# Low-rank conditional adapters: a closing product for every tile, or a fold into the heads' matrix for every batch

## The chip, the cores and the metric

The kernel runs on one core of one Trainium2 chip. The metric is the device time of one execution in microseconds; lower is better. Before the change the runs take 332.83, 332.95 and 333.03 us, with a median of 332.95. The engines are named as in the profile: PE (matrix products) and PEld (its weight loads), DVE (vector), ACT (scalar), POOL (GpSimd) and SP (the queue that issues most transfers).

## The reference

Eight batches of 512 rows, all in fp32. Each batch b has an adapter of rank 16, chosen by an index out of 32. The first layer is a full matrix plus bias plus the batch's adapter; the second routes each row to the best of 8 experts, each of rank 16. The cut code below leaves out how the inputs are drawn.

```
base_out = einsum('bti,oi->bto', x, W) + b            # W: 2048 x 2048
A, Bm = lora_As[adapter_mapping], lora_Bs[adapter_mapping]
y = base_out + 2.0 * einsum('btr,bro->bto', einsum('bti,bir->btr', x, A), Bm)

logits = einsum('bsd,ed->bse', y, route_w)            # 8 experts
topk_v, topk_idx = top_k(logits, 1)
weight = one_hot(topk_idx[..., 0], 8) * topk_v
h = einsum('bsd,erd->bser', y, A_ffn)                 # 8 x 16 = 128 columns
out = x + einsum('bser,eor->bso', weight[..., None] * h, B_ffn)
```

Only 136 columns of y are wanted, 128 of h and 8 logits, "the heads" in what follows. With proj the 2048 x 136 matrix of A_ffn and route_w, the heads of a row are x (W' proj) + b proj + 2 (x A)(Bm proj).

## The kernel before

**W stage (`chunk_w`, `fold_w`, loop over oc = 0 to 15).** W is loaded in 16 pieces of 128 rows. ACT and DVE bring each piece into blocks, and PE adds W' proj up in six PSUM tiles `pc` (3, 3, 3, 3, 3 and 1 blocks of 128 x 136). At oc = 15 the groups are copied, by ACT and DVE in turn, into the tiles `cms`. Between the pieces other work is put in by hand, in the order of the loop's `if oc == ...` lines: the adapters B are gathered by POOL (`load_adapters_b`), turned on PE in four groups (`turn_adapters`) and multiplied by proj (`project_adapters`, giving G, 128 x 136: 8 batches x 16 rows); G goes to DRAM and comes back in four copies into `g4`. The adapters A are gathered in four quarters (`load_adapters_a`), turned by DVE into `ad_aT`, and 16 columns of each batch are put beside W' proj by `place_a`. The first row tiles of x are loaded, moved in blocks (`shuffle`, on POOL and ACT) and turned by DVE (`turn_x`).

**Main loop (line 557).** There are 32 tiles of 128 rows, four to a batch, and each takes two iterations n, with t, h = divmod(n, 2). In each iteration the engines get this work, each in this order:

- PE: `heads` for half of the tile's 16 blocks of x, with the columns of `cms`: 16 of A and 136 of W' proj, 152 in all, into `ph`. Then `delta` for an earlier half tile (`piece(n)` is the half tile of n - 3): two products of 512 columns into one of two PSUM buffers `po`. In odd iterations then `add_low`, the closing product: the 16 columns x A of the tile, turned, times `g4`, added into `ph`; in even ones `turn_heads`, the transposition of the routed heads of the tile before.
- DVE: in even iterations `route` (five instructions on the 136 columns of the tile before, in PSUM); then `add_delta` for the half tile of the last iteration (x plus `po`, in place, 128 x 1024), `turn_x` for half of the next tile, and in odd iterations `turn_low`, which brings the 16 columns x A into four masked copies and turns them.
- ACT: in odd iterations `keep_heads`, the copy `whT` that `delta` multiplies; then its share of the moves of x for a later pair of tiles (`shuffle_slot`). POOL has the other moves, and once a batch `place_a` for the next batch but one.
- SP: the stores of finished tiles, and after them the load of the pair of tiles that takes the freed buffer. There are five buffers of two tiles.

An engine takes its work in the order in which it is written; semaphores between engines are set by the framework from the tiles read and written. PSUM has two buffers for `ph`, two of two banks for `po`, and two small ones (`ps_s`), which `pw` of `turn_heads` uses.

Of the kernel before, what the change touches and what calls it, by code (L numbers as in the profile page):

```python
# [9 lines left out]
F32 = mybir.dt.float32  # L10
# [8 lines left out]
def kernel(  # L19
# [28 lines left out]

    nc = tc.nc
# [19 lines left out]
    NA = NP + R  # L69
# [7 lines left out]
    dram = ctx.enter_context(tc.tile_pool(name="dram", bufs=1, space=bass.MemoryType.DRAM))  # L77
# [54 lines left out]
    for _ in range(14):  # L132
# [5 lines left out]
    quad_i = const.tile([P, NQ, 2], I32, name="quad_i")  # L138
    nc.gpsimd.iota(
        quad_i, pattern=[[1 - 2 * R * NQ, NQ], [-R * NQ, 2]], base=0, channel_multiplier=NQ  # L140
    )

# [14 lines left out]
    ad_ar = raw[:, 1, :].rearrange("p (k d) -> p k d", k=NQ)  # L157
# [3 lines left out]
    it_f = const.tile([P, B], F32, name="it_f")  # L161

    def load_adapters_b():

        nc.vector.tensor_scalar(it_f, it_i, float(R), None, ALU.mult)
# [3 lines left out]
        brow_f = const.tile([P, 1], F32, name="brow_f")  # L169
# [11 lines left out]
    def load_adapters_a():  # L181

        quad = const.tile([P, B], F32, name="quad")
        nc.vector.tensor_copy(quad, quad_i.rearrange("p i h -> p (i h)"))
        nc.vector.tensor_tensor(quad, quad, mask, ALU.mult)
        base = const.tile([P, 1], F32, name="base")
        nc.vector.tensor_reduce(base, quad, AX.X, ALU.add)
        odd = const.tile([P, 1], F32, name="odd")
        nc.vector.tensor_reduce(
            odd, mask.rearrange("p (i h) -> p h i", h=2)[:, 1, :], AX.X, ALU.add  # L190
        )
        it_q = const.tile([P, NQ, 2], F32, name="it_q")
        nc.vector.tensor_scalar(
            it_q, it_f.rearrange("p (k h) -> p k h", h=2), float(NQ), None, ALU.mult
        )
        arow_f = const.tile([P, NQ], F32, name="arow_f")
        nc.vector.tensor_tensor(arow_f, it_q[:, :, 1], it_q[:, :, 0], ALU.subtract)
        nc.vector.tensor_scalar(arow_f, arow_f, odd, base, ALU.mult, ALU.add)
        nc.vector.tensor_tensor(arow_f, arow_f, it_q[:, :, 0], ALU.add)
        arow_i = const.tile([P, NQ], I32, name="arow_i")  # L200
        nc.vector.tensor_copy(arow_i, arow_f)
        for m in range(NQ):
            nc.gpsimd.indirect_dma_start(
                out=ad_ar[:, m, :],
                out_offset=None,
                in_=cond_a.rearrange("s (i d) -> (s i) d", i=NQ),
                in_offset=bass.IndirectOffsetOnAxis(ap=arow_i[:, m : m + 1], axis=0),
            )

    one = const.tile([P, NQ, Q], F32, name="one")  # L210
    own4 = const.tile([P, NQ], F32, name="own4")
    hls = []

    def fill_constants():

        nc.vector.memset(one, 0.0)
        nc.vector.memset(one[:, :, R : R + 1], 1.0)

        nc.vector.tensor_reduce(
            own4, mask.rearrange("p (g h) -> p g h", h=2), AX.X, ALU.add  # L220
        )
        for k in range(2):
            h = const.tile([P, NQ, Q], F32, name=f"hls_{k}")
            nc.vector.memset(h, 0.0)
            nc.vector.tensor_copy(h[:, :, R : R + 1], own4.unsqueeze(2))
            hls.append(h)
# [5 lines left out]
    cms = [const.tile([P, n, NA + R], F32, name=f"cm_{n}") for n in (JC, NJ - JC)]  # L232

    def cm(j):
        return cms[j // JC][:, j % JC, :]

    def place_a(b, copy):
        for k, part in enumerate(cms):
            n = part.shape[1]
            copy(part[:, :, ds(b % 2 * NA, R)], ad_aT[:, ds(k * JC, n), ts(b, R)])  # L240

    ad_aT = const.tile([P, NJ, P], F32, name="ad_aT")
    ad_bT = tpool.tile([P, NJ, P], F32, tag="t", name="ad_bT")
    g4 = const.tile([P, B, NP], F32, name="g4")
    GRP = 512 // NP
    groups = [(j0, min(GRP, NJ - j0)) for j0 in range(0, NJ, GRP)]

    def turn(dst, src, h):

        nc.vector.transpose(  # L250
            dst[:, ts(h, HJ), :].rearrange("p j (g t) -> p g j t", t=Q),
            src.rearrange("p g (j a) -> p g j a", a=Q)[:, :, ts(h, HJ), :],
        )

# [48 lines left out]
    def fold_w(oc):  # L303
        for q, (pc, (j0, n)) in enumerate(zip(pcs, groups)):
# [11 lines left out]
            if oc == NO - 1:  # L316
                copy = nc.scalar.copy if q % 2 == 0 else nc.vector.tensor_copy
                copy(cms[j0 // JC][:, ds(j0 % JC, n), R:NA], pc[:, :n, :])

# [19 lines left out]
    g_dram = dram.tile([P, NP], F32, name="g_dram")  # L339

    def project_bias():

        pb = ps_s.tile([P, NP], F32, tag="s", name="pb")
        nc.tensor.matmul(
            pb, one.rearrange("p i s -> p (i s)"), bp, start=True, stop=True
        )
        nc.vector.tensor_copy(g4, pb.unsqueeze(1).to_broadcast([P, B, NP]))

    def project_adapters():
# [7 lines left out]
        nc.sync.dma_start(out=g_dram, in_=g_sb)  # L357
        for i in range(NQ):
            nc.sync.dma_start(
                out=g4[ds(i * Q, R)], in_=g_dram.rearrange("(b r) e -> r b e", r=R)  # L360
            )

    chunk_w(0)
    for oc in range(NO):
        if oc + 1 < NO:
            chunk_w(oc + 1)
        fold_w(oc)
# [6 lines left out]
        if 8 <= oc < 12:  # L374
            turn_adapters(oc - 8)
        if oc in (9, 10):
            fold_bias(range(8 * (oc - 9), 8 * (oc - 8)))
        if oc == 8:
            load_x(0)
            shuffle(0, moves[6:], nc.gpsimd.tensor_copy)  # L380
        if oc == 11:
            nc.sync.dma_start(out=fb, in_=ffn_b)
            load_x(1)
            load_x(2)
            project_bias()
        if oc in (10, 11):
            turn(ad_aT, ad_ar, oc - 10)
        if oc == 11:
            for b in range(2):
                place_a(b, nc.vector.tensor_copy)  # L390
        if oc == 12:
            project_adapters()
        if oc in (12, 13, 14):
            shuffle(0, moves[2 * (oc - 12) : 2 * (oc - 11)], nc.scalar.copy)
        if oc == 14:
            for h in range(2):
# [4 lines left out]
    xpool2 = ctx.enter_context(tc.tile_pool(name="xpool2", bufs=1))  # L401
    xpools.update({k: xpool2 for k in range(3, XB)})
# [3 lines left out]
    hT_tiles = {}  # L406
# [8 lines left out]
    def heads(t, j0, j1):  # L415
        s = batch_of(t) % 2
        if j0 == 0:

            pool, tag = (ps_h, "h") if t else (ps_s, "s")
            ph_tiles[t] = pool.tile([P, 512], F32, tag=tag, name=f"ph_{t}")[:, :NA]  # L420
        for j in range(j0, j1):
# [3 lines left out]
                cm(j)[:, ds(s * R, NA)],  # L425
# [4 lines left out]
    def turn_low(t):  # L430

        s = batch_of(t) % 2
        h = hls[t % 2]
        nc.vector.tensor_tensor(
            h[:, :, :R],
            ph_tiles[t][:, ds(s * NP, R)].unsqueeze(1).to_broadcast([P, NQ, R]),
            own4.unsqueeze(2).to_broadcast([P, NQ, R]),
            ALU.mult,
        )
        hT = small.tile([P, P], F32, tag="hT", name=f"hT_{t}")  # L440
        nc.vector.transpose(hT, h.rearrange("p g s -> p (g s)"))  # L441
        hT_tiles[t] = hT

    def add_low(t):
        b = batch_of(t)
        nc.tensor.matmul(  # L446
            ph_tiles[t][:, ds((1 - b % 2) * R, NP)],
# [199 lines left out]
```

## Time and profile before

| | before |
|---|---|
| median of the runs | 332.95 us |
| profiled execution | 332.04 us |
| its span, first to last instruction | 330.3 us |
| W stage, end of the last `pc` product | 72.4 us |
| PE busy from 81.01 to 316.24 us (235.23 us) | 235.23 us |
| heads, `ph` L422 | 1024 records, 142.6 us |
| closing products, `ph` L446 | 64 records, 12.7 us |
| DVE pair behind them, L434 and L441 | 32 x 188 ns, 32 x 311 ns |
| `route`, five lines | 167, 226, 162, 500 and 292 ns each |
| delta products, `po` L515 | 240 records, 112.8 us |
| granted PE clock | 0.999 |

A group's busy time is the time in which at least one of its instructions runs; matmuls overlap, so their single durations are longer than the distance from one to the next. The chain of waits follows the work that ended last from the end back to the start; where the chain stays on PE from one line to the next, PE had no gap there. "Released by" or an arrow names the instruction that ended an idle time.

### The profile page before, as it was taken

The page shows a single profiled execution, that of the slowest core. Times are in us where ns is not written, and L with a number is a line of the kernel's source. Part 1 is how long each engine was busy: PE and PEld are TensorE (multiplying, and loading weights), DVE is VectorE, ACT ScalarE, POOL GpSimd, SP SyncE. Part 2 cuts the span into 40 slices and gives each one's busy share as a digit, 9 for nine tenths or more (in the row PEclk, how much of TensorE's full clock was granted, in tenths as well). Part 3 has the DMA queues.
Part 4 walks back from the last instruction along what each step waited for, and adds up shares of the span by engine and source line. Part 5 has one row for each costly group of instructions (what it writes and reads, how often), then busy time and mean ns, then how long its engine had stood idle before and what let it go on. Part 6 is the DMA issues. An engine that isn't in the chain of part 4 may idle for free.

```text
span 330.3 us, 5132 instructions
## 1 busy us (share of the span) xinstructions
PE 324.2 (98%) x1968; PEld 260.8 (79%) x1968; DVE 234.3 (71%) x429; ACT 171.0 (52%) x193; POOL 136.7 (41%) x148
## 2 busy tenths in 40 slices
PE   8999999999999999999999999999999999999994
PEld 8999999998777777777777777777777777777762
DVE  1132376566877877887878888878888787787764
ACT  3234136647766538565656575667565665740000
POOL 1002403999882609264535536254808070700000
PEclk9999999999999999999999999999999999999999
DMA  7999999958643394857676675859493939433336
GB/s 286 347 409 418 419 406 424 419 220 342 270 167 131 119 386 157 360 179 329 217 293 243 267 279 229 297 215 359 167 372 168 373 153 383 191 127 129 128 159 222
DMA packets 16200, 88.83 MB, mean 269 GB/s; under 512 B 1824, under 2 KB 4784, under 8 KB 5936
## 3 DMA queue, kind: packets, MB, share of 16 engines
q1 hardware_dynamic: 14832, 85.80, 66.1%
q0 software_dynamic: 496, 2.11, 1.6%
q10 hardware_dynamic: 848, 0.61, 0.6%
q8 instruction: 15, 0.25, 0.3%
q14 instruction: 9, 0.07, 0.1%
HBM read 54.88 MB, written 33.62 MB: 268 GB/s over the span
## 4 chain that ended last, share of the span: by engine, by line
PE 94%; DMA 3%; SPq 0%; ACT 0%; DVE 0%; issue 0%; DVEq 0%; ACTq 0%
PE ph L422 40%; PE po L515 31%; PE pc L308 16%; DMA w<-in_w_dram 3%; PE ph L446 2%; PE pg L353 1%; PE pw L477 1%; PE pe_o L515 1%; PE pbT L335 1%; PE pe_h L515 1%; ACT wv L297 0%; DVE x L528 0%; PE pe_s L515 0%; SPq L102 0%; SPq L96 0%
## 5 line engine op out<-in xcount | busy, mean ns | idle before, releaser
L265 POOL COPY xq<-x 32x1024 f32<-32x1024 f32 x121 | 126.7, 1047 | 118.9 <-DMA x<-in_x_dram 67.6
L265 ACT COPY xq<-x 32x1024 f32<-32x1024 f32 x135 | 140.9, 1043 | 20.3 <-DMA x<-in_x_dram 11.0
L422 PE MATMUL ph<-cm,xT 128*128 128x152 f32 x1024 | 142.6, 293 | 0.0
L422 PEld LDWEIGHTS ph<-cm,xT 128*128 128x128 f32 x1024 | 135.1, 190 | 8.7 <-issue 8.7
L515 PE MATMUL po<-fb,whT 128*128 128x512 f32 x240 | 112.8, 592 | 0.0
L250 DVE STREAM_TRANSPOSE xT<-xq 128x1024 f32<-128x1024 f32 x64 | 78.8, 1235 | 0.9 <-POOL xq L265 0.9
L528 DVE TENSOR_TENSOR x<-x,po 128x1024 f32<-128x1024 f32 x60 | 72.6, 1210 | 5.2 <-PE po L515 5.0
L515 PEld LDWEIGHTS po<-fb,whT 128*128 128x128 f32 x240 | 42.0, 190 | 28.7 <-issue 28.7
L308 PE MATMUL pc<-pj,wv 128*128 128x136 f32 x512 | 60.7, 279 | 0.5 <-ACT wv L297 0.5
L308 PEld LDWEIGHTS pc<-pj,wv 128*128 128x128 f32 x512 | 59.8, 190 | 0.8 <-ACT wv L297 0.7
L482 ACT COPY whT<-pw 128x128 f32<-128x128 f32 x32 | 8.5, 266 | 85.8 <-PE pw L477 85.8
L297 DVE COPY wv<-w 128x1024 f32<-128x1024 f32 (+1 forms) x17 | 12.4, 737 | 31.2 <-DMA w<-in_w_dram 19.8
L297 ACT COPY wv<-w 128x1024 f32<-128x1024 f32 (+1 forms) x17 | 16.8, 997 | 27.9 <-DMA w<-in_w_dram 25.3
L459 DVE TENSOR_REDUCE top<-ph 128x1 f32<-128x8 f32 x32 | 5.3, 167 | 36.5 <-PE ph L446 36.5
L446 PEld LDWEIGHTS ph<-g,hT 128*128 128x128 f32 x64 | 12.0, 190 | 15.0 <-issue 11.7
L465 DVE TENSOR_SCALAR rw<-rank,win,top 128x8 f32<-128x8 f32 x32 | 16.0, 500 | 1.2
L446 PE MATMUL ph<-g,hT 128*128 128x136 f32 x64 | 12.7, 280 | 0.0
L173 POOL DMA_INDIRECT raw<-in_cond_b_dram,brow_i x1 | 1.5, 1462 | 24.3 <-DVE brow_i L172 24.3
L477 PEld LDWEIGHTS pw<-ident,wh 128*128 128x128 f32 x32 | 4.5, 140 | 7.9 <-issue 5.7
L441 DVE STREAM_TRANSPOSE hT<-hls 128x128 f32<-128x128 f32 x32 | 10.0, 311 | 1.1
L467 DVE TENSOR_TENSOR wh<-ph,rw 128x128 f32<-128x128 f32 x32 | 9.3, 292 | 1.1
L477 PE MATMUL pw<-ident,wh 128*128 128x128 f32 x32 | 8.8, 274 | 0.0
(69 smaller groups left out, 90.8 us busy)
## 6 DMA issues: line engine op xcount, KB each, us to landing
x<-in_x_dram SPq DMA_DIRECT2D x32, 1024.0 KB, 8.9
out_dram<-x SPq DMA_DIRECT2D x30, 1024.0 KB, 4.9
w<-in_w_dram SPq DMA_DIRECT2D x16, 1024.0 KB, 11.7
out_dram<-x SPq DMA_DIRECT2D x6, 256.0 KB, 2.6
fb<-in_ffn_b_dram SPq DMA_DIRECT2D x1, 1024.0 KB, 15.0
pj<-in_proj_dram SPq DMA_DIRECT2D x2, 272.0 KB, 11.0
g<-g_dram SPq DMA_DIRECT2D x4, 68.0 KB, 2.8
out_dram<-x ACTq DMA_DIRECT2D x1, 256.0 KB, 2.5
```

The lines of the kernel that those rows point to most:

```text
L250: nc.vector.transpose(dst[:, ts(h, HJ), :].rearrange("p j (g t) -> p g j t", t=Q), src.rearrange("p g (j a) -> p g j a", a=Q)[:, :, ts(h, ...
L265: copy(xq_tiles[u][ts(i, Q), :, g, :], x_tiles[u][ts(g, Q), :, ts(i, DQ)])
L297: copy(dst[:, ts(k, n)], wr[:, ds(h * HJ + k * n, n)])
L308: nc.tensor.matmul(pc[:, k, :], wv_tiles[oc, h][:, j, :], pj[:, oc, :], start=(oc == 0 and k == 0), stop=(oc == NO - 1), skip_group_check= ...
L422: nc.tensor.matmul(ph_tiles[t], xT_tiles[t][:, j, :], cm(j)[:, ds(s * R, NA)], start=(j == 0), stop=(j == NJ - 1),)
L441: nc.vector.transpose(hT, h.rearrange("p g s -> p (g s)"))
L446: nc.tensor.matmul(ph_tiles[t][:, ds((1 - b % 2) * R, NP)], hT_tiles.pop(t), g4[:, b, :], start=False, stop=True, skip_group_check=True,)
L465: nc.vector.tensor_scalar(rw, rank, win, top, ALU.is_equal, ALU.mult)
L467: nc.vector.tensor_tensor(wh.rearrange("p (e r) -> p e r", r=R), ph[:, :ER].rearrange("p (e r) -> p e r", r=R), rw.unsqueeze(2).to_broadca ...
L477: nc.tensor.transpose(pw, wh_tiles.pop(t), ident)
L515: nc.tensor.matmul(part, whT_tiles[t], fb[:, ds(c, n)], start=True, stop=True)
L528: nc.vector.tensor_tensor(xs, xs, part, ALU.add)
```

## The change

The adapters are no longer applied to every tile. For each batch the product A G is formed, 2048 x 136, and added to W' proj, so that the heads' matrix `ms[b % 2]` holds both: heads have 136 columns, and `turn_low`, `add_low` and the four masked copies go. W' proj is kept in `cs`. The bias' row is held in `c0b` and added by DVE as the first instruction of `route`, which now reads the sum `hl` in SBUF and stands in the odd iteration of its own tile.

A G has 16 terms, or 32 for a pair of batches with the other batch's rows of `g4` at nothing. So each of the 16 blocks is a product over 32 rows (`tile_position=(q * 32, 0)`), and A's blocks are spread over the four groups of rows (`spread_a`, 20 copies on POOL and 4 on ACT into `ad_q`); G is brought to all four groups by four products with an identity of 32 rows (`spread_g`), in place of the way through DRAM. `adapter_products` takes the groups of rows in turn, each with its own bank. For batch 0 this happens in the W stage in three bunches (`first_products`), and W' proj is added at oc = 15: ACT copies each group into `cs`, DVE adds it to `ms[0]`.

For batches 1 to 7 `fold_adapter` runs in the loop, in the odd iteration of the third tile of the batch before. Its 16 products use both `po` buffers and both small ones. DVE adds two pieces to `cs` straight out of PSUM; ACT copies four pieces out, and POOL adds `cs` to them. No `delta` is issued in that iteration; the next one issues two, and the `add_delta` of the first of them comes after `turn_x` on DVE. A is gathered whole by one gather in place of four.

```
     def load_adapters_a():
...
+        arow_i = const.tile([P, 1], I32, name="arow_i")
+        nc.vector.tensor_copy(arow_i, brow_f)
+        nc.gpsimd.indirect_dma_start(
+            out=ad_ar,
+            out_offset=None,
+            in_=cond_a,
+            in_offset=bass.IndirectOffsetOnAxis(ap=arow_i, axis=0),
+        )
...
+    half = const.tile([P, 2], F32, name="half")
+    def fill_constants():
         nc.vector.tensor_reduce(
-            odd, mask.rearrange("p (i h) -> p h i", h=2)[:, 1, :], AX.X, ALU.add
+            half, mask.rearrange("p (k h) -> p h k", h=2), AX.X, ALU.add
...
-        for m in range(NQ):
-            nc.gpsimd.indirect_dma_start(
-                out=ad_ar[:, m, :],
-                out_offset=None,
-                in_=cond_a.rearrange("s (i d) -> (s i) d", i=NQ),
-                in_offset=bass.IndirectOffsetOnAxis(ap=arow_i[:, m : m + 1], axis=0),
-            )
...
-    cms = [const.tile([P, n, NA + R], F32, name=f"cm_{n}") for n in (JC, NJ - JC)]
-    def cm(j):
-        return cms[j // JC][:, j % JC, :]
-    def place_a(b, copy):
-        for k, part in enumerate(cms):
-            n = part.shape[1]
-            copy(part[:, :, ds(b % 2 * NA, R)], ad_aT[:, ds(k * JC, n), ts(b, R)])
-    ad_aT = const.tile([P, NJ, P], F32, name="ad_aT")
+    parts = (JC, NJ - JC)
+    cs = [const.tile([P, n, NP], F32, name=f"c_{n}") for n in parts]
+    ms = {0: [const.tile([P, n, NP], F32, name=f"m0_{n}") for n in parts]}
+    ad_q = const.tile([P, NQ, 5, P], F32, name="ad_q")
+    def spread_a(q, k, copy):
+        src = ad_ar[ts(k, Q), :].rearrange("p (i j a) -> p j i a", i=NQ, a=Q)
+        dst = ad_q[ts(q, Q), k].rearrange("p j (i a) -> p j i a", a=Q)
+        copy(dst[:, :3], src[:, ds(3 * q, 3)])
+        if q < 2:
+            copy(dst[:, 3:], src[:, ds(JC + 2 * q, 2)])
...
+    eyes = const.tile([P, NQ, Q], F32, name="eyes")
+    nc.vector.tensor_reduce(
+        eyes[:, 0, :], ident.rearrange("p (q c) -> p c q", c=Q), AX.X, ALU.add
+    )
+    nc.vector.tensor_copy(eyes[:, 1:, :], eyes[:, :1, :].to_broadcast([P, NQ - 1, Q]))
...
-    def fold_w(oc):
+    def fold_w(oc, within=None):
         for q, (pc, (j0, n)) in enumerate(zip(pcs, groups)):
             for k in range(n):
...
             if oc == NO - 1:
-                copy = nc.scalar.copy if q % 2 == 0 else nc.vector.tensor_copy
-                copy(cms[j0 // JC][:, ds(j0 % JC, n), R:NA], pc[:, :n, :])
+                k, jk = divmod(j0, JC)
+                c, m = (part[k][:, ds(jk, n), :] for part in (cs, ms[0]))
+                nc.scalar.copy(c, pc[:, :n, :])
+                nc.vector.tensor_tensor(m, m, c, ALU.add)
+            if q == 2 and within:
+                within()
...
         pb = ps_s.tile([P, NP], F32, tag="s", name="pb")
-        nc.tensor.matmul(
-            pb, one.rearrange("p i s -> p (i s)"), bp, start=True, stop=True
-        )
-        nc.vector.tensor_copy(g4, pb.unsqueeze(1).to_broadcast([P, B, NP]))
+        nc.tensor.matmul(pb, warm, bp, start=True, stop=True)
+        nc.vector.tensor_copy(c0b, pb)
...
         nc.vector.tensor_scalar(g_sb, pg, COND_SCALING, None, ALU.mult)
-        nc.sync.dma_start(out=g_dram, in_=g_sb)
-        for i in range(NQ):
-            nc.sync.dma_start(
-                out=g4[ds(i * Q, R)], in_=g_dram.rearrange("(b r) e -> r b e", r=R)
+    def spread_g(ks):
+        for k in ks:
+            pq = ps_s.tile([P, NP], F32, tag="s", name=f"pq_{k}")
+            nc.tensor.matmul(
+                pq,
+                eyes[ts(k, Q)].rearrange("p q c -> p (q c)"),
+                g_sb[ts(k, Q), :],
+                start=True,
+                stop=True,
+                tile_position=(k * Q, 0),
             )
+            for h in range(2):
+                nc.vector.tensor_scalar(
+                    g4[:, 2 * k + h, :], pq, half[:, h : h + 1], None, ALU.mult
+                )
+    pieces = [(0, 3 * q, 3, q) for q in range(NQ)] + [(1, 2 * q, 2, q) for q in range(2)]
+    def adapter_products(b, some, banks):
+        for n in range(3):
+            for z in some:
+                part, _, nj, q = pieces[z]
+                if n < nj:
+                    nc.tensor.matmul(
+                        banks[z][:, n, :],
+                        ad_q[ts(q, Q), b // 2, 3 * part + n, :],
+                        g4[ts(q, Q), b, :],
+                        start=True,
+                        stop=True,
+                        tile_position=(q * Q, 0),
+                    )
+    def place(b, z):
+        part, j0, nj, _ = pieces[z]
+        return (t[part][:, ds(j0, nj), :] for t in (ms[b % 2], cs))
+    def first_products(some):
+        banks = {
+            z: ps_s.tile([P, GRP, NP], F32, tag="s", name=f"pa_{z}") for z in some
+        }
+        adapter_products(0, some, banks)
+        for z in some:
+            m, _ = place(0, z)
+            nc.vector.tensor_copy(m, banks[z][:, : pieces[z][2], :])
...
-        fold_w(oc)
+        fold_w(
+            oc,
+            {
+                13: lambda: spread_g((2, 3)),
+                14: lambda: first_products((2, 3)),
+            }.get(oc),
+        )
...
-        if 8 <= oc < 12:
-            turn_adapters(oc - 8)
+        for g in {8: (0,), 9: (1, 2), 10: (3,)}.get(oc, ()):
+            turn_adapters(g)
         if oc in (9, 10):
             fold_bias(range(8 * (oc - 9), 8 * (oc - 8)))
         if oc == 8:
             load_x(0)
+            for k in range(NQ):
+                for q in range(3):
+                    spread_a(q, k, nc.gpsimd.tensor_copy)
...
         if oc == 11:
+            for k in range(NQ):
+                spread_a(3, k, nc.scalar.copy)
...
-        if oc in (10, 11):
-            turn(ad_aT, ad_ar, oc - 10)
-        if oc == 11:
-            for b in range(2):
-                place_a(b, nc.vector.tensor_copy)
-        if oc == 12:
             project_adapters()
         if oc in (12, 13, 14):
             shuffle(0, moves[2 * (oc - 12) : 2 * (oc - 11)], nc.scalar.copy)
+        if oc == 12:
+            spread_g((0, 1))
+        if oc == 13:
+            first_products((0, 1))
         if oc == 14:
+            first_products((4, 5))
             for h in range(2):
                 turn_x(0, h)
...
     def heads(t, j0, j1):
...
             nc.tensor.matmul(
                 ph_tiles[t],
                 xT_tiles[t][:, j, :],
-                cm(j)[:, ds(s * R, NA)],
+                m[j // JC][:, j % JC, :],
                 start=(j == 0),
                 stop=(j == NJ - 1),
             )
-    def turn_low(t):
-        s = batch_of(t) % 2
-        h = hls[t % 2]
-        nc.vector.tensor_tensor(
-            h[:, :, :R],
-            ph_tiles[t][:, ds(s * NP, R)].unsqueeze(1).to_broadcast([P, NQ, R]),
-            own4.unsqueeze(2).to_broadcast([P, NQ, R]),
-            ALU.mult,
-        )
-        hT = small.tile([P, P], F32, tag="hT", name=f"hT_{t}")
-        nc.vector.transpose(hT, h.rearrange("p g s -> p (g s)"))
-        hT_tiles[t] = hT
-    def add_low(t):
-        b = batch_of(t)
-        nc.tensor.matmul(
-            ph_tiles[t][:, ds((1 - b % 2) * R, NP)],
-            hT_tiles.pop(t),
-            g4[:, b, :],
-            start=False,
-            stop=True,
-            skip_group_check=True,
-        )
...
     def route(t):
-        s = batch_of(t) % 2
-        ph = ph_tiles.pop(t)[:, ds((1 - s) * R, NP)]
+        hl = small.tile([P, NP], F32, tag="hl", name=f"hl_{t}")
+        nc.vector.tensor_tensor(hl, ph_tiles.pop(t), c0b, ALU.add)
         top = small.tile([P, 1], F32, tag="top", name=f"top_{t}")
-        nc.vector.tensor_reduce(top, ph[:, ER:NP], AX.X, ALU.max)
+        nc.vector.tensor_reduce(top, hl[:, ER:NP], AX.X, ALU.max)
...
+    def fold_adapter(b):
+        banks = {}
+        for z in range(0, 4, 2):
+            po = ps_o.tile([P, HN, 512], F32, tag="o", name=f"pa_{b}_{z}")
+            for k in range(2):
+                banks[z + k] = po[:, k, : GRP * NP].rearrange("p (j e) -> p j e", e=NP)
+        for z in (4, 5):
+            banks[z] = ps_s.tile([P, GRP, NP], F32, tag="s", name=f"pa_{b}_{z}")
+        adapter_products(b, range(4), banks)
+        adapter_products(b, (4, 5), banks)
+        for z in range(6):
+            m, c = place(b, z)
+            pa = banks[z][:, : pieces[z][2], :]
+            if z < 2:
+                nc.vector.tensor_tensor(m, c, pa, ALU.add)
+            else:
+                nc.scalar.copy(m, pa)
+        for z in range(2, 6):
+            m, c = place(b, z)
+            nc.gpsimd.tensor_tensor(m, m, c, ALU.add)
     def turn_heads(t):
         pw = ps_s.tile([P, P], F32, tag="s", name=f"pw_{t}")
@@ -554,43 +582,46 @@
         load_x(u)
     for n in (-2, -1):
         shuffle(*shuffle_slot(n), nc.gpsimd.tensor_copy)
+    def folds(n):
+        t, h = divmod(n, 2)
+        b, k = divmod(t, TPB)
+        return b + 1 if h == 1 and k == 2 and 0 <= b < B - 1 else None
...
-        if h == 0 and 0 < t <= NT:
-            route(t - 1)
         tp, hp = piece(n - 1)
-        if tp >= 0:
+        if tp >= 0 and not folds(n - 1):
             add_delta(tp, hp)
         turn_x(t + 1, h)
         if h == 1 and 0 < t <= NT:
             keep_heads(t - 1)
-        u, ms = shuffle_slot(n)
-        shuffle(u, ms, nc.gpsimd.tensor_copy if n == 2 else nc.scalar.copy)
+        if folds(n):
+            fold_adapter(folds(n))
         if h == 1 and t < NT:
-            turn_low(t)
-        last = n in (2 * NT - 1, 2 * NT)
...
+            route(t)
+        u, ms_u = shuffle_slot(n)
+        shuffle(u, ms_u, nc.gpsimd.tensor_copy if n == 2 else nc.scalar.copy)
+        if folds(n):
+            pass
+        elif n == 2 * NT:
+            delta(*piece(n), lambda: turn_heads(t - 1))
+        else:
+            if folds(n - 1):
+                delta(*piece(n - 1))
+                add_delta(*piece(n - 1))
+            if piece(n)[0] >= 0:
+                delta(*piece(n))
+            if n == 2 * NT - 1:
                 add_delta(*piece(n), 1)
-        elif piece(n)[0] >= 0:
-            delta(*piece(n))
-        if h == 1 and 0 < t < NT and not last:
-            add_low(t)
-        if h == 1 and t < NT:
-            b, k = divmod(t, TPB)
-            if k == 0 and 0 < b < B - 1:
-                place_a(b + 1, nc.gpsimd.tensor_copy)
-        if h == 0 and 1 < t <= NT and not last:
+        if h == 0 and 1 < t < NT:
             turn_heads(t - 1)
         tq, hq = piece(n - 5)
         u, k = divmod(tq, TPU)
```

## Prediction

> **What bounds the kernel now.** I read the page's first two parts (busy times, slices, granted clock), then a table of windows, then the chain of waits in order of time.
>
> ```profile
> PE 324.2 (98%) x1968; PEld 260.8 (79%) x1968; DVE 234.3 (71%) x429; ACT 171.0 (52%) x193; POOL 136.7 (41%) x148
> PEclk9999999999999999999999999999999999999999
> ```
> ```profile
> 81.01:316.24 235.23, 235.23 (x1276) 176.35 (x1276) 189.00 (x329) 136.40 (x153) 105.17 (x111) 1.00 0.61 238
> ```
>
> The columns of the second fence are window, length, busy time of PE, PE's weight loads, DVE, ACT and POOL, granted clock, DMA share, GB/s. From 81 us to 316 us PE is busy without a gap at the full clock, and DVE for 189 of 235 us. So a nanosecond of matmul counts in full, and nothing else counts until PE waits for it.
>
> ```profile
> 165.84 0.11 PE pw L477
> 165.95 2.07 PE ph L422 x16
> 168.02 1.72 PE po L515 x4
> 169.74 0.23 PE ph L446 x2
> 169.97 2.07 PE ph L422 x16
> 172.03 1.72 PE po L515 x4
> ```
>
> This is one row tile in the chain: 0.11 + 2.07 + 1.72 + 0.23 + 2.07 + 1.72 = 7.92 us. Eight products of the heads make 16 records: one fp32 matmul is two records, each with its own weight load. A record of 152 columns takes 2.07/16 = 0.129 us. The W stage is also solid PE work and gives the price at 136 columns:
>
> ```profile
> 53.87 3.71 PE pc L308 x32
> 57.57 3.71 PE pg L353 x32
> ```
>
> 3.71/32 = 0.116 us a record, 0.232 us a matmul.
>
> **What the change takes away.** Heads: 512 products, 1024 records, each 0.129 - 0.116 = 0.0132 us shorter: 13.5 us. Closing products: 32 x 0.23 = 7.4 us. Together **20.9 us** on PE, 0.65 us a tile. The DVE pair behind them goes too (188 + 311 ns by the groups), and one addition of 128x136 out of PSUM comes (like the 292 ns of the wh line): DVE falls from about 6.4 us a tile by 0.2, against a PE tile of 7.27 us. DVE doesn't become the bound on average.
>
> **What it adds on PE in the loop.** Seven times (batches 1 to 7) 16 products of 32 rows by 136 columns. No such product is in the trace. Dear end: each costs what a full one does, 16 x 0.232 = 3.71 us. Cheap end: four row groups run fully side by side; the pieces have 3, 3, 3, 3 and 2, 2 products, so five rounds, 5 x 0.232 = 1.16 us. In between: in every stretch of the trace PE's records stand in the order of the program, and the two records of one product use the same rows. If that order holds, the first record of a product can run beside the last of the one before, and no more: 17 x 0.116 = 1.97 us. I take **1.97 us**, because all rows here show records in order; 7 x 1.97 = 13.8 us (8.1 to 26.0).
>
> The Trainium skill has rules on both sides. "TensorE: Matmul & The Clock Gate", Part 3, gives a measured speedup of 3.07 for four row tiles at 512 columns; 3.71 us would become an estimated 1.21 us a batch, 5.3 us less over seven than my sum. The same page (LDWEIGHTS) says that a load of 32 rows takes as long as one of 128, which speaks for the dear end if loads take turns. "TensorEngine Tiling (Array Packing)", Key Properties, says that a change of tiling mode drains the array; that speaks against the change. No run here shows any of the three.
>
> Going into and out of these products may cost a stop. Bounds from rows: a product whose weight load isn't covered costs 0.16 us more than a covered one (the last transposition at 321.19 us, 0.27 against 0.11 us). Above, a 136-column record lasts 0.279 us in the groups and is followed after 0.116, so waiting for its end adds 0.163, and an uncovered load of 0.190 more: 0.35. The low end is nothing. I take **0.25 us** for each of 14 crossings: 3.5 us (0 to 4.9).
>
> **A new wait in the loop.** In the folding iteration, POOL gets four additions (two of 408, two of 272 columns) ahead of its last two moves of the next pair of tiles; ACT gets four copies out of PSUM ahead of its last two. Prices:
>
> ```profile
> L240 POOL COPY cm<-ad_aT 128x192 f32<-128x192 f32 x6 | 2.1, 344 | 0.4
> L318 ACT COPY cm<-pc 128x408 f32<-128x408 f32 x3 | 1.5, 500 | 4.8 <-PE pc L308 4.8
> L240 POOL COPY cm<-ad_aT 128x64 f32<-128x64 f32 x6 | 1.4, 231 | 0.0
> ```
>
> POOL's copies cost 0.175 us + 0.88 ns an element: 0.53 and 0.41 us for 408 and 272. Additions read two tensors. Cheap end: the copies' price, 1.9 us for the four; dear end: twice, 3.8 us. Count from E, the end of the products. ACT's first copy is done at E + 0.2 (its product ended before E), the last at E + 1.6. POOL's additions then end between E + 2.1 and E + 4.05, its two moves (1.05 us each) between 4.2 and 6.15. Only then can DVE turn the next tile (1.24 us), and in this iteration the addition of the postponed delta (1.21 us) stands behind that turn on DVE: done between E + 6.75 and E + 8.7. That addition frees the PSUM buffer which PE wants for the delta of the iteration after. PE has by then one crossing, heads, two deltas, a transposition and heads: 0.25 + 1.85 + 3.44 + 0.11 + 1.85 = E + 7.5. So PE waits 0 to 1.2 us. I take the additions nearer the dear end, since no row has POOL read two tensors at the price of one: **1.0 us** a batch, 7.0 us (0 to 8.4). Behind that turn on DVE stand also the next deltas and the routing; DVE has a fifth of its time free and catches up in two iterations.
>
> "GPSIMD Engine Reference" in the Trainium skill says that additions of two inputs run at about half of VectorE's rate on that engine and gives 4497 ns for 2048 fp32 columns; that would be an estimated 3.0 us for the four, and a wait of some 0.4 us, 2.8 us in all where I have 7.0. No run here shows it.
>
> **What it adds before the loop.** That stage is solid PE too. 4 spreading and 16 folding products in five bunches, pairs of row groups: by the in-between rule 20 x 0.116 + 5 x 0.116 = 2.9 us (2.3 for ten rounds of 0.232; 4.6 for 20 single ones). Ten crossings: 2.5 us (0 to 3.5). At its end heads wait for six ACT copies and now six DVE additions of SBUF tensors. After the fourth group PE has four products left, 0.93 us, against 0.50 (ACT) + 0.58 (DVE's 408-column copy): 0.2 us late. But POOL moves x all this time, and DVE's W copy goes from 0.69 to 1.53 us then:
>
> ```profile
> 33.38 0.69 DVE L297 COPY wv<-w 128x1024 f32<-128x1024 f32 x1 [3.01 <-PE pc L308]
> ...
> 58.35 1.53 DVE L297 COPY wv<-w 128x1024 f32<-128x1024 f32 x1
> ```
>
> I take **1.0 us** (0.2 to 2).
>
> **At nothing.** POOL's 20 spreading copies: 12 x 0.51 + 8 x 0.40 = 9.3 us. POOL waits for x until 54.99 us anyway; the A gather was last seen landing at 50.5, so x's moves slip by 5 us at most, to 71.7, and the first turn to 74.1, with PE's fold ending at 72.4 + 5.4 = 77.8. Without that cover each microsecond would delay the first heads by as much. ACT's four spreads (about 2 us) stand in an iteration in which it is busy for 1.6 of 3.7 us. DVE loses two turns and five placing copies (some 5 us) and gains 8 spreads, 6 copies and the sum of two masks, about 6 us in a stage where it is busy 28 of 58. The bias products and the 16 transpositions only move. On the queues: SP loses the store of G and four loads that stood ahead of x's tiles 3 and 4 (72.48 to 74.30 us), POOL three of four gathers of the same bytes; x's loads gain up to 2 us there. In the loop the narrowest place is ACT's moves at 282.22 us, which waited for x and ended 2.1 us before PE would have missed whT; four iterations shorter by 0.33 us leave 0.8 us.
>
> **Sum.** -13.5 - 7.4 + 13.8 + 3.5 + 7.0 + 2.9 + 2.5 + 1.0 = **+9.8 us**. The profiled execution took 332.04 us (span 330.3 and 1.7 around it); the median of the runs is 332.95. By the sum the profile of after has a span near 340.1 and the median is **342.7 us**. Within the case, no crossing cost and no POOL wait give 329.7; the dear ends of both and of the startup 347.5.
>
> **Rivals.** *The row groups take turns.* Products at 3.71 a batch and 4.6 before the loop: 12.2 + 1.7 = 13.9 us more, 356.6; without the POOL wait 349.6. For it: two weight loads to each short product, and no row with two products at once. Against: weight loads already overlap products in all of the trace.
>
> *Four at a time, faster.* Products at 1.16 and 2.3: five rounds. With the additions cheap enough for POOL's chain to end before E + 7.5: -20.9 + 8.1 + 3.5 + 2.3 + 2.5 + 1.0 = -3.5 us, **329.4 us**. It decides below a price of a folded batch of (20.9 - 2.3 - 2.5 - 1.0)/7 = 2.2 us on PE, crossings and waits included; full overlap and two crossings are 1.66. For it: pieces go to four different banks and to rows that don't touch. Against: the two records of a product follow each other.
>
> *Pairs, but POOL not late.* The forecast without its wait: **335.7 us**; for it, POOL is idle for 59% and its moves before the additions run ahead.
>
> **How the numbers follow.** Forecast 0.36 (342.7), turns 0.30, four at a time 0.20, pairs without a wait 0.14. The measurement tells about 0.2%, 0.7 us, from no change. Faster: 0.17 of the four (the rest for its having the wait) and 0.06 of the two cases of pairs with cheap crossings: 0.23. Same: 0.05. Slower: 0.72. Range 327.5 to 354: it takes in the fast case and its crossings below my value, and most of the dear one; 330 to 347.5 is the forecast's own.
>
> **What will show it.** The folding products' records and the gap from heads to the next heads: 2 us (pairs), 1.2 (four), 3.7 (turns). PE idle beside them: crossings. A PE wait for a DVE addition to x two iterations later, with POOL's additions and moves ahead of the DVE turn: the new wait. Heads at 1.85 us for 16 records. I am wrong above all if a folded batch costs PE less than 2.2 us, or if another engine (ACT with whT, x's landing) holds PE in most tiles.

## Result and profile after

The changed kernel takes 341.14 us (median; 339.94 to 342.87) against 332.89 before: a ratio of 1.0252 with a 95% interval of 1.0204 to 1.03, **slower by 8.2 us**. The profiled execution took 340.57 us, its span is 338.5 against 330.3. The page's first part, and one window of the loop, with the columns as in the prediction:

```profile
PE 321.7 (95%) x2168; PEld 253.3 (75%) x2168; DVE 253.8 (75%) x410; ACT 184.1 (54%) x228; POOL 165.6 (49%) x180
PEclk9999999999999999999999999999999999999999
```
```profile
169.70:327.10 157.40, 152.47 (x949) 111.49 (x950) 136.09 (x209) 91.26 (x114) 77.62 (x78) 1.00 0.62 241
```

PE has less work than before (321.7 against 324.2 us busy) and yet ends later: in the loop, where it had no gap, it is now idle for 4.9 of 157.4 us at the same full clock. The list of what PE waited for (total us, times, longest) names the places:

```profile
PE po L543 <- DVE x L556: 7.7, 7, 1.1
PE pw L505 <- DVE wh L472: 2.1, 2, 1.5
PE ph L452 <- DVE m L297: 1.1, 3, 0.4
```

Seven waits of 1.1 us for a DVE addition to x: one for each folded batch. The other two rows stand at the start of the loop, but for one wait of some 0.5 us for `wh` at 119 us, after the first fold. The chain of waits goes through one fold so:

```profile
158.53 1.86 PE ph L452 x16
160.38 0.98 PE pa L361 x24
161.38 0.51 ACT m L498
162.03 3.55 POOL m L501 x4
165.66 1.01 POOL xq L242
166.71 1.05 POOL xq L242
167.82 1.13 issue
168.95 1.19 DVE x L556
170.28 1.96 PE po L543 x4
```

The heads take 1.86 us for 16 records, as predicted for 136 columns. The products' first 24 records take 0.98 us. Then the chain leaves PE: ACT's first copy, POOL's four additions (3.55 us), POOL's two moves of x behind them, DVE's turn (here "issue", 1.13 us; DVE's rows have it from 167.78 to 169.03), DVE's delayed addition, and only then the delta. By POOL's and DVE's groups:

```profile
L501 POOL TENSOR_TENSOR m<-m,c 128x408 f32<-128x408 f32 x14 | 14.4, 1052 | 49.0 <-ACT m L498 42.9 <-issue 6.1
L501 POOL TENSOR_TENSOR m<-m,c 128x272 f32<-128x272 f32 x14 | 10.7, 786 | 0.0
L297 DVE TENSOR_TENSOR m<-m,c 128x408 f32<-128x408 f32 x5 | 4.8, 1020 | 0.0
L472 DVE TENSOR_TENSOR wh<-hl,rw 128x128 f32<-128x128 f32 x32 | 20.7, 648 | 1.1
L466 DVE SCALAR_TENSOR_TENSOR key<-hl,top,rank 128x8 f32<-128x8 f32 x32 | 11.2, 350 | 1.1
```

POOL's additions are at the dear end of the prediction (2 x 1.05 + 2 x 0.79 = 3.68 us; 3.8 said). Three DVE instructions are slower than the rows they were priced by: the 408-column additions at the end of the W stage (1.02 us; 0.58 for the copies of before), and the routing's last product and comparison (648 and 350 ns; 292 and 226 before). DVE's busy time rises from 234.3 to 253.8 us.

**Where the 8.2 us of span went.** A batch in the loop takes 31.89 us (heads of the folding tile at 158.53 us, of the next at 190.42) against 31.64 before. The part before the first heads is 4.9 us longer (they start at 72.2 before; the fold of W ends near 77.1 now). From there to the heads of the third tile takes 13.0 us (77.1 to 90.1) against 10.6 before, though 1.3 us of heads and closing products are gone: a loss of 3.75 us (the last kernel below takes 9.24, 77.09 to 86.33). The rest is in the loop.

### The profile page after: what moved, and what is told of

Same layout as the page of the kernel before. It is cut to its first block, busy times and chain, and to the rows that moved or that the text cites. A ratio compares the mean times of both kernels' runs of the same rounds, so it can differ in the third digit from the quotient of the medians.

```text
span 338.5 us, 5603 instructions
## 1 busy us (share of the span) xinstructions
PE 321.7 (95%) x2168; PEld 253.3 (75%) x2168; DVE 253.8 (75%) x410; ACT 184.1 (54%) x228; POOL 165.6 (49%) x180
## 4 chain that ended last, share of the span: by engine, by line
PE 64%; POOL 13%; DVE 10%; issue 6%; DMA 5%; ACT 1%; POOLq 0%; DVEq 0%; ACTq 0%
PE ph L452 23%; PE po L543 21%; PE pc L285 13%; POOL m L501 7%; POOL xq L242 5%; DVE x L556 4%; DMA w<-in_w_dram 3%; PE pa L361 2%; DVE xT L220 2%; DMA pj<-in_proj_dram 2%; DVE m L297 1%; PE pg L330 1%; PE pe_o L543 1%; ACT m L498 1%; PE pw L505 1%
## 5 line engine op out<-in xcount | busy, mean ns | idle before, releaser
L452 PEld LDWEIGHTS ph<-m,xT 128*128 128x128 f32 x1024 | 125.0, 190 | 20.0 <-issue 14.0
L452 PE MATMUL ph<-m,xT 128*128 128x136 f32 x1024 | 130.2, 280 | 1.1 <-DVE m L297 1.1
L556 DVE TENSOR_TENSOR x<-x,po 128x1024 f32<-128x1024 f32 x60 | 71.4, 1199 | 3.8 <-PE po L543 3.6
L501 POOL TENSOR_TENSOR m<-m,c 128x408 f32<-128x408 f32 (+1 forms) x28 | 24.8, 919 | 49.0 <-ACT m L498 42.9
L472 DVE TENSOR_TENSOR wh<-hl,rw 128x128 f32<-128x128 f32 x32 | 20.7, 648 | 1.1
L498 ACT COPY m<-pa 128x408 f32<-128x408 f32 (+1 forms) x28 | 10.4, 457 | 17.6 <-PE pa L361 17.6
L470 DVE TENSOR_SCALAR rw<-rank,win,top 128x8 f32<-128x8 f32 x32 | 18.9, 592 | 1.2
L361 PE MATMUL pa<-g,ad_q 32*128 32x136 f32 x256 | 12.7, 288 | 0.0
L466 DVE SCALAR_TENSOR_TENSOR key<-hl,top,rank 128x8 f32<-128x8 f32 x32 | 11.2, 350 | 1.1
L361 PEld LDWEIGHTS pa<-g,ad_q 32*128 32x128 f32 x256 | 10.6, 184 | 1.3
```

Source lines behind the costliest of these rows:

```text
L361: nc.tensor.matmul(banks[z][:, n, :], ad_q[ts(q, Q), b // 2, 3 * part + n, :], g4[ts(q, Q), b, :], start=True, stop=True, tile_position=(q ...
L452: nc.tensor.matmul(ph_tiles[t], xT_tiles[t][:, j, :], m[j // JC][:, j % JC, :], start=(j == 0), stop=(j == NJ - 1),)
L470: nc.vector.tensor_scalar(rw, rank, win, top, ALU.is_equal, ALU.mult)
L472: nc.vector.tensor_tensor(wh.rearrange("p (e r) -> p e r", r=R), hl[:, :ER].rearrange("p (e r) -> p e r", r=R), rw.unsqueeze(2).to_broadca ...
L498: nc.scalar.copy(m, pa)
L501: nc.gpsimd.tensor_tensor(m, m, c, ALU.add)
```

## Experiments

**One: the moves of x ahead of the fold.** In the folding iteration POOL and ACT have their moves for the next tiles before the products, where they waited for PE anyway.

```
         if folds(n):
+            u, ms_u = shuffle_slot(n)
+            shuffle(u, ms_u, nc.scalar.copy)
             fold_adapter(folds(n))
...
-        u, ms_u = shuffle_slot(n)
-        shuffle(u, ms_u, nc.gpsimd.tensor_copy if n == 2 else nc.scalar.copy)
+        if not folds(n):
+            u, ms_u = shuffle_slot(n)
+            shuffle(u, ms_u, nc.gpsimd.tensor_copy if n == 2 else nc.scalar.copy)
```

> The folding iteration's last moves of x (two on ACT, two on POOL) are issued ahead of the fold's products, copies and additions; nothing else changes. Theory (POOL's two moves stand behind its four additions, so DVE's turn and the delayed addition behind it come late, and PE waits 1.1 us plus an uncovered weight load of 0.2 in each of seven batches): the PE waits on the delayed addition go from 7.7 us in all to under 1, and the time falls by 8 to 9 us, to about 332.5 us. Rival (the wait comes from DVE having too much in that stretch, whatever POOL does): the waits shrink by less than a third and the time stays above 338. Rival (ACT's two moves ahead of its copies now hold up the PSUM buffers): PE waits for ACT copies appear and most of the gain is lost, 337 to 341.

Measured: 330.47 us (330.38 to 330.75), a ratio to before of 0.9941 (0.9930 to 0.9953). The waits of the delta on DVE are gone from the list. The chain of waits through the same fold:

```profile
155.31 1.86 PE ph L452 x16
157.16 1.36 PE pa L361 x32
158.52 2.05 PE ph L452 x16
160.57 3.43 PE po L543 x8
164.00 0.11 PE pw L505
164.12 1.86 PE ph L452 x16
165.97 1.72 PE po L543 x4
```

The chain stays on PE. POOL's additions are as long as ever (3.54 us in its rows) and nobody waits for them. So the order of a few instructions was worth 10.7 us by the medians (341.14 to 330.47), 9.9 us by the profiled spans (338.5 to 328.6), and turned the change from a loss into a gain of 0.6%. Of the 9.9 us, the seven waits with the uncovered weight load beside each make 9.3 (7 x 1.33, worked out under three); the 8 to 9 us expected left out the wait after the first fold, which went too. No ACT wait took the place of the old one.

**Two: the same wait cut on DVE.** POOL stays late, but the addition no longer stands behind the turn.

```
-        turn_x(t + 1, h)
+        if not folds(n - 1):
+            turn_x(t + 1, h)
...
                 add_delta(*piece(n - 1))
+                turn_x(t + 1, h)
```

> Only in the iteration after a fold, DVE's turn of the next tile is put behind the addition of the postponed delta; POOL keeps its additions ahead of its moves. Theory (it is the order on DVE that lets a late POOL reach PE): the addition no longer waits for POOL, the PE waits of 7.7 us go to under 1.5, time about 332.5 to 333.5 us, though POOL's additions and moves end as late as before. Rival (the turn is needed as early as it stood; what is late is the turn itself, by way of the next heads): the wait of PE moves from the delta to heads on the turned tile, and the time stays above 338.

Measured: 333.22 us (332.26 to 334.56), ratio to before 1.0025 (1.0012 to 1.0038). DVE's timeline after a fold (start, length, instruction, in brackets the idle time before it and who ended it):

```profile
163.07 1.22 DVE L556 TENSOR_TENSOR x<-x,po 128x1024 f32<-128x1024 f32 x1 [0.59 <-PE po L543]
165.31 1.25 DVE L220 STREAM_TRANSPOSE xT<-xq 128x1024 f32<-128x1024 f32 x1 [1.02 <-POOL xq L242]
```

DVE still waits 1.02 us for POOL, but with the addition done before, PE doesn't. So both links are needed for the loss: POOL late, and the delayed addition behind the turn. This cure leaves a batch at 30.75 us (products at 157.91 and 188.66) against 30.57 (157.16 and 187.73) with the first one, which is 1.3 us over seven batches; the medians are 2.75 us apart, and the rest of that was not followed up.

**Three: no folds in the loop.** `folds` returns None and all tiles use `ms[0]`: the adapters of batches 1 to 7 are left out.

> Leaves out the folds of batches 1 to 7: all tiles are multiplied by the matrix of batch 0, and the loop has the deltas in their usual place. It prices all that a fold costs. Theory (1.5 us of products and crossings and 1.3 us of waiting a batch): 7 x 2.8 = 20 us less than the changed kernel, about 321 us, with a tile of 7.26 us in the loop. Rival (the loop lost time by its other rearrangements too, such as the routing in the odd iteration): the loop's tile stays above 7.5 us and the time above 327.

Measured: 319.44 us, one run. From 170 to 310 us PE is busy throughout:

```profile
170.00:310.00 140.00, 140.00 (x786) 101.44 (x785) 122.94 (x193) 80.23 (x92) 58.07 (x56) 1.00 0.67 260
```

A batch takes 29.01 us (heads at 151.84 and, four tiles on, at 180.85). So in this stretch nothing else in the new loop holds PE. With the 30.56 us of a batch in the first experiment (155.31 to 185.87), a fold's **products and crossings cost 30.56 - 29.01 = 1.55 us, and the wait 31.89 - 30.56 = 1.33 us**.

**Four to six: the order of the products.** First, piece by piece in the changed kernel:

```
-        for n in range(3):
-            for z in some:
+        for z in some:
+            for n in range(3):
```

> The 16 products of a fold (and those of batch 0) are ordered piece by piece, so that neighbours use the same 32 rows, apart from the change of piece. Theory (four row groups run side by side because neighbours use different rows; 24 records take about 1.0 us): by the piece order the records run one after another, 32 x 0.116 less some overlap at the five changes of piece, 3.1 to 3.7 us a batch in place of 1.4; PE time of the products rises by 12 to 16 us over seven batches and by 1 to 2 in the W stage, part of it given back by a shorter wait on POOL (up to 6 us), time 347 to 354 us. Rival (a product over 32 rows is simply shorter than one over 128): records stay at 0.04 us apart, time unchanged within 2 us of 341.

Measured: 347.26 us, one run. The time fell inside the range, at its low edge, but neither number of its working did: the products took 2.04 us, neither 3.1 nor 1.36, and the waits grew from 7.7 to 9.6 us in place of shrinking. The counts of records that touch a window of 0.06 us show it, first for the kernel after, then for this one (window, length, PE busy, count in brackets):

```profile
160.54:160.60 0.06, 0.06 (x8) 1.00 0.64 273
160.77:160.83 0.06, 0.06 (x12) 1.00 0.64 273
160.89:160.95 0.06, 0.06 (x12) 1.00 1.29 546
```
```profile
162.57:162.63 0.06, 0.06 (x4) 1.00 1.29 546
162.86:162.92 0.06, 0.06 (x6) 1.00 1.93 819
163.15:163.21 0.06, 0.06 (x7) 1.00 1.93 819
```

A record lasts 0.274 us, and full products, one after another, show 3 in such a window. In the changed kernel 12 are under way, four times as many: four products at a time. Ordered by pieces there are 6 to 7, about two at a time. Since the wait on POOL blurs the time, two orders were run again on the first experiment's kernel: by pieces, and the first four pieces in two pairs.

```
-        adapter_products(b, range(4), banks)
+        adapter_products(b, (0, 1), banks)
+        adapter_products(b, (2, 3), banks)
```

> The kernel with the moves ahead of the fold (330.5 us, 1.36 us for a fold's 32 records), with the products ordered piece by piece, so that neighbours mostly use the same 32 rows. With no wait on POOL left, the time shows the price of the order alone. Theory (PE starts a record whose rows are free although one before it in the program still waits for its own rows, but sees only a short way ahead; 2.04 us a fold in the earlier run of this order): 0.7 us x 7 more in the loop and 0.5 to 1 us in the W stage, 335.5 to 336.5 us. Rival (strict program order, overlap only where the piece changes, 27 steps of 0.116): 3.1 us a fold, 12 us more in the loop, above 342.

> The kernel with the moves ahead of the fold, with the first four pieces in two pairs (products of pieces 0 and 1 in turn, then of 2 and 3): neighbours use different rows, but only two groups of rows stand near one another in the program. Theory (PE sees some records ahead, so the second pair starts before the first is through): between 1.4 and 1.7 us a fold, 331 to 333 us. Rival (only what stands next in the program can run beside: two at a time, 6 + 6 + 4 steps of 0.116 in place of 6 + 4): 2.0 us a fold, 335 us.

Measured: by pieces 335.39 us (335.24 to 335.51), 4.9 us more than with all four in turn; in pairs 330.66 us (330.52 to 330.81), the same. Both are a little under their ranges (335.5 and 331). The chain of waits has a fold, by pieces and then in pairs, as below; the third view counts records in a window of the fold in pairs.

```profile
189.60 2.04 PE pa L361 x31
```
```profile
187.52 1.36 PE pa L361 x27
```
```profile
188.22:188.28 0.06, 0.06 (x12) 1.00 1.93 819
```

(The chain does not pass through all 32 records.) With pairs in turn, strict program order would allow two at a time and 16 steps of 0.116, 1.9 us; PE does it in the 1.36 us of four, and here too 12 records are under way at once. So it starts products on free rows that stand some places further on in the program; in this, PE is an exception to the sentence, given with the kernel before, that an engine takes its work in the order in which it is written. How far it looks was not measured; six records of one piece in a row are too many for full overlap.

**Seven: the start of the loop.**

```
-                nc.vector.tensor_tensor(m, m, c, ALU.add)
+                nc.vector.tensor_tensor(m, m, pc[:, :n, :], ALU.add)
...
-            first_products((4, 5))
             for h in range(2):
                 turn_x(0, h)
+            first_products((4, 5))
```

> At the end of the W stage DVE adds each group of W' proj to the first matrix straight out of PSUM (not from ACT's copy in SBUF), and turns x's first tile ahead of the last two copies of products. Theory (the start of the loop lost 3.7 us: the additions took 1.02 us each, not 0.58, because both operands lay in SBUF while POOL moved x, and they stood behind the turns; heads and then the first transposition waited for DVE): additions near 0.58 us, the three gaps in the first heads (1.1 us) and most of the 1.5 us wait of the transposition go, time 2.5 to 3.5 us less than the changed kernel, 337.5 to 338.6 us. Rival (the start waits for POOL's and ACT's moves of x, DVE only passes it on): additions shorter, but the second tile's heads start within 1 us of before, time above 340.

Measured: 339.08 us (337.78 to 339.52), ratio to before 1.0180 (1.0161 to 1.0198): 2.1 us less than the changed kernel, under the range's edge of 2.5. The additions take 578 ns in place of 1020:

```profile
L297 DVE TENSOR_TENSOR m<-m,pc 128x408 f32<-128x408 f32 x5 | 2.9, 578 | 0.4
```

The gaps in the first heads are gone; the first transposition still waits 0.5 us, and a wait of 1.1 us for ACT's `whT` is new.

**Eight: the routing in PSUM.**

```
-        hl = small.tile([P, NP], F32, tag="hl", name=f"hl_{t}")
-        nc.vector.tensor_tensor(hl, ph_tiles.pop(t), c0b, ALU.add)
+        hl = ph_tiles.pop(t)
+        nc.vector.tensor_tensor(hl, hl, c0b, ALU.add)
```

> The sum of heads and bias is written back in place in PSUM instead of into SBUF, so that the routing's instructions have one operand in PSUM as they had before the change. Theory (DVE instructions with two SBUF operands are held up while POOL works): the last product of the routing goes from 648 back to about 292 ns and the comparison from 350 to about 226, DVE busy falls by some 15 us; PE is held by DVE only at the start, so the time falls by 1 to 2 us, to 339 to 340 us. Rival (they are slow for another reason, such as the place in the iteration): durations stay above 500 and 300 ns and the time is the same within 0.5 us.

Measured: 338.57 us (337.96 to 340.55), ratio 1.0190 (1.0167 to 1.0213): 2.6 us less, a little over the range. The groups:

```profile
L472 DVE TENSOR_TENSOR wh<-ph,rw 128x128 f32<-128x128 f32 x32 | 9.3, 292 | 1.1
L466 DVE SCALAR_TENSOR_TENSOR key<-ph,top,rank 128x8 f32<-128x8 f32 x32 | 7.2, 226 | 1.1
```

Both are back at the durations of before, and DVE is busy for 240.6 in place of 253.8 us. Here and in the experiment before it, one operand moved from SBUF to PSUM removes the slowness. No run left out POOL's work by itself, but the rows separate it. In the changed kernel, the 14 last products (L472) with no POOL work beside them take 0.29 us each, as before, and the nine that lie wholly beside it 0.80 to 1.15 us; with the operand in PSUM all 32 take 0.29 us, though 19 of them lie wholly beside POOL's work. The five 408-column additions show the same: 1.14, 1.41 and 1.41 us while POOL moves x, 0.57 us for the two after POOL's move has ended at 79.8 us. So in these rows the slowness needs both: two operands in SBUF, and POOL at work beside them.

**Nine: all three cures together.**

> The moves ahead of the fold, the additions out of PSUM with the earlier turn at the start, and the routing in PSUM, together. Theory (three separate causes, nothing else late): 10.7 us from the first and 3 to 3.7 us from the others, which share the start: 326.5 to 328 us, 1.5 to 2% below the kernel before the change. Rival (a next wait shows, such as x's landing or ACT's whT in the shorter tile): the sum falls short by 2 us or more, 329 to 330.5 us.

Measured: **326.77 us** (326.16 to 327.01), ratio to before 0.9819 (0.9806 to 0.9832), inside the expected range. Its page:

```profile
PE 318.4 (98%) x2168; PEld 252.2 (78%) x2168; DVE 238.2 (73%) x410; ACT 184.5 (57%) x228; POOL 164.7 (51%) x180
```
```profile
169.70:313.20 143.50, 143.50 (x907) 105.50 (x906) 120.81 (x196) 86.21 (x108) 71.96 (x72) 1.00 0.63 244
```

PE has no gap in the loop again, and the change is worth 1.8%: 14.4 us between the same mathematics with its instructions in two orders and some DVE operands in two places.

## Why the prediction was right, and where it was not

The forecast (342.7, slower, range 327.5 to 354) held, and its new wait is shown to be the cause of the sign. But the total also agrees by luck, because errors of both signs met: 6.4 us too much for products and crossings, some 5 us too little for the wait and the start of the loop.

| step | predicted | measured | from |
|---|---|---|---|
| heads of 136 columns, closing products | -20.9 | -21.0 | 8 batches x (29.01 - 31.64) (three, before) |
| products and crossings, 7 folds | 13.8 + 3.5 | 10.9 | 7 x 1.55 (one, three) |
| wait on the POOL chain, 7 folds | 7.0 | 9.3 | 7 x 1.33 (one, three) |
| W stage | 2.9 + 2.5 | 4.9 | 72.2 against 77.1 us |
| start of the loop | 1.0 | 3.75 | 13.0 against 9.25 us to the third tile |
| sum | +9.8 | +7.85 | span: +8.2 |

- **Savings:** right to 0.1 us, since the price at 136 columns stood in the W stage of the same trace.
- **Products, wrong:** the step "the first record of a product can run beside the last of the one before, and no more" failed. It took the order of records in stretches where all products use all rows for a rule about products that don't share rows. Four run side by side; 1.36 us from the first to the next heads' first record, near the rival's 1.16. Crossings cost about 0.2 us a fold beyond that, and the returns in the W stage 0.2 us each (18 records of W in 2.28 us where 18 x 0.116 is 2.09), under the 0.25 taken for every one. The row that the Trainium skill's "TensorE: Matmul & The Clock Gate", Part 3, put against my term was the better guide: 16 x 0.232 = 3.71 us against 1.36 is a factor of 2.7 at 136 columns, beside its 3.07 at 512.
- **The new wait, right in place and mechanism:** every link of the chain was as written (additions 3.68 us for 3.8). With E at the next heads' first record, 161.7 us, the addition was done at E + 8.4 and PE there at E + 7.45; the prediction had PE at E + 7.5 and a wait of 1.0. The size was 1.33 and not 1.0: the wait itself was 1.1, and the prediction left out a weight load of some 0.24 us that goes uncovered after it (the delta takes 1.96 us in place of 1.72). The Trainium skill's "GPSIMD Engine Reference", "Elementwise — side-by-side cycle accounting", would have made the additions an estimated 3.0 us and the wait 0.4; its two-input slowness is confirmed (1.05 us for 408 columns, where DVE's unhindered addition takes 0.57), but these short additions took 3.68.
- **The rivals.** "Turns" (349.6 to 356.6) fell with the twelve records under way. "Four at a time" was right about the products; its break-even of 2.2 us a fold on PE, waits included, decided: the fold costs 1.55 us without the wait and 2.88 with it, and the kernels lie on the two sides of before as that says. With the measured 4.9 and 3.75 us ahead of the loop's third tile in place of the 5.8 taken there, the break-even is (21.0 - 8.65)/7 = 1.76 us, still between the two. "Pairs without a wait" (335.7) had the products' price wrong like the forecast: with the wait removed, the first experiment took 330.47 us.
- **Start of the loop, mis-sized:** it was priced for the additions alone. Missed were the turns of x ahead of them on DVE, and that the routing, now with both operands in SBUF, becomes slow at the same moment (the first transposition waited 1.55 us). The row of a W copy that went from 0.69 to 1.53 us beside POOL was quoted, but not carried over to the routing, which I had priced at its old duration; so DVE, forecast to fall by 0.2 us a tile, rose instead.
- **At nothing, right:** POOL's spreading and the gathers delayed nothing (in the last kernel the chain of waits stays on PE from the W stage into the loop); x's landing and ACT's `whT` hold PE nowhere in the loop of the last kernel.

## What to carry to other kernels

When work is put into an engine's queue, look first at what was next in that queue and follow it to the bound engine: here additions whose result was ready at 165.6 us and used at 172.1 stood ahead of two copies that were needed at once, and swapping them was worth more than the change had cost. Price a product on a part of the array from a run, not from full products: with neighbours on different rows 16 of them took 1.36 us in place of 3.71. And when a result moves from PSUM to SBUF, price its readers again.

## What the runs showed of the hardware

- Products over 32 rows on four groups of rows run four at a time in fp32, though each is two records: 12 records of 0.274 us under way against 3 for full products. Two pairs in turn run as fast as four in turn (1.36 us a fold, 12 records under way), and piece by piece takes 2.04 us: PE takes products on free rows ahead of earlier ones that wait for theirs.
- On DVE, an operand moved from SBUF into PSUM made instructions faster: 1020 to 578 ns (128 x 408), 648 to 292 ns (128 x 128), 350 to 226 ns (128 x 8). With both operands in SBUF, those with no POOL work beside them were as fast (0.57 us for 128 x 408, 0.29 us for 128 x 128).
- POOL adds two SBUF tensors at 1.96 ns a column ((1052 - 786)/136), 2.2 times the 0.88 of its copies before.
